# Denominators of 45 group halves by transpose and reduction on VectorE, in place of a matmul with ones

## The chip, the core and the metric

The kernel runs on one core of a Trainium2 chip. The metric is the device time of one execution in microseconds (us). The engines are TensorE (PE, with its weight loads PEld), VectorE (DVE), ScalarE (ACT), GpSimd (POOL) and SyncE (SP), which issues nearly all transfers. Each engine works through its own list of instructions in order, and semaphores order the lists against each other.

## The reference

A decoder block in fp32 on x (4, 1024, 512) with a context (4, 1024, 384). Three sublayers, each on a layernorm and each added to x:

- Self attention, 16 heads of 32. Scores of `x@Wi` against `x@Wo`, softmax over keys, times an aperture per query and an expression gate per key, and then normalized again by the sum over keys plus 1e-8:

```python
attn = attn_align * aperture.transpose(0, 2, 1)[..., :, None] * expression.transpose(0, 2, 1)[..., None, :]
attn = attn / (attn.sum(axis=-1, keepdims=True) + 1e-08)
```

  So for each head and query two sums over the keys are needed: that of the exps, and that of the exps weighted by the expression gate.
- Cross attention to the context, 16 heads of 32: an ordinary softmax, one sum of exps for each head and query.
- A network of 64 units with 16 inner relus each.

## The kernel before

**Units, halves and group halves.** There are eight attention units u: phase 0 (self attention) for the four batches, u = 0 to 3, then phase 1 (cross attention), u = 4 to 7. A unit has two halves hf of 512 queries, and a half has four groups g of four heads. The 64 triples (u, hf, g) are the group halves. Each has eight steps kt of 128 keys. `run` interleaves the steps with items from `beside`: projections, layernorms, output projections and the network of the neighbouring units. The order of every engine is the order in which the program writes it.

**One step.** `scores` (L633) computes two score tiles (two heads each, 128 keys x 1024, L641), and ACT turns each into an `e` tile by exp (L647). There are six buffers for `e`, so three steps' worth. In the next step `times` (L704) multiplies the `e` tiles with the values into `av` (L707).

**The sums over keys.** They come from three places:
- DVE adds `e` tiles over the eight steps into `es` (L669, L671): in phase 0 for the first two heads, in phase 1 of units 4 to 6 for both pairs. In phase 0 it also adds the gated exps of the first two heads into `eg` (L679; ACT starts it, L678).
- In phase 0 the other two heads get both sums from PE: rounds of four matmuls into `sm`, one round for two steps, with ones and the gate as weights (L717).
- For the group halves in the table `gated` (L625), DVE does the first 4 or 6 steps of those two heads, into `exa` (L685, L687) and `exb` (L692, started by ACT, L691), and PE takes these up in one round.

DVE's tiles are sums over steps only; the 128 keys of a step still lie in 128 partitions. `normalize` (L730) runs after the last step of a group half (it falls in step 0 of the next), copies `av` away (L733) and in phase 0 `sm` (L735), and one step later `add_up` (L743) sums over partitions: a round of four matmuls with `ones` as weights (L746), a copy (L747), and transfers through memory that bring the sums into a tile `c` of 128 partitions x 16 queries. Two steps later `divide` (L767) forms the reciprocals and sends them out and back, spread over partitions (`recb`), and two steps after that `multiply` (L795) applies them (L797). Unit 7 has a different split (`shared`, `added_up`).

**Buffers that matter.** `es0`, `es1`, `exa`, `exb`, `both` and `recb` have one buffer each; `eg` uses `es1`. The two tiles `cs_` are used in turn. PSUM has two score tiles, two banks `f` for everything else, and one each for `av` and `sm`. DVE frees a bank `f` where it adds the output projection to the residual (L891) or scales the values (L565); ACT frees most others.

Of the kernel before, what the change touches and what calls it, by code (L numbers as in the profile page):

```python
# [10 lines left out]
F32 = mybir.dt.float32  # L11
U32 = mybir.dt.uint32
AF = mybir.ActivationFunctionType
ALU = mybir.AluOpType
AX = mybir.AxisListType

P = 128
B, T, D = 4, 1024, 512
H, DH = 16, 32
NPR = H // 2  # L20
HG = 4
# [4 lines left out]
HALF = 512  # L26
M, INNER = 64, 16
# [12 lines left out]
NB = 32  # L40
# [29 lines left out]
def moderate_path(tc: tile.TileContext, a: dict, out: bass.AP, flag: bass.AP):  # L70
    nc = tc.nc
    x = a["x"]
    with ExitStack() as st:
        enter = st.enter_context
        const = enter(tc.tile_pool(name="mconst", bufs=1))
        dram = enter(tc.tile_pool(name="mdram", bufs=1, space=bass.MemoryType.DRAM))
# [4 lines left out]
        p1 = enter(tc.tile_pool(name="mp1", bufs=1))  # L81
        p2 = enter(tc.tile_pool(name="mp2", bufs=2))
# [35 lines left out]
        iap_d = [[dram.tile([H, HALF], F32, tag=f"iap_{b}_{i}", name="iap_d") for i in range(2)] for b in range(B)]  # L118
        sum1_d = [dram.tile([HG, HALF], F32, tag=f"sum1_{i}", name="sum1_d") for i in range(4)]
        sum2_d = [dram.tile([2, HG, HALF], F32, tag=f"sum2_{i}", name="sum2_d") for i in range(4)]  # L120
        rec_d = [dram.tile([HG, HALF], F32, tag=f"rec_{i}", name="rec_d") for i in range(4)]
        wout_d = dram.tile([P, NC, D], F32, name="wout_d")

# [2 lines left out]
        fixed = const.tile([P, 3], F32, name="fixed")  # L126
        ones, share, power = (fixed[:, i : i + 1] for i in range(3))
        pick = const.tile([P, 3], F32, name="pick")
        nc.gpsimd.memset(pick, 0.0)
        nc.gpsimd.memset(pick[:, 1:2], 1.0)  # L130
        for one, is_ in ((ones, 1.0), (power, -0.5), (share, 1.0 / M)):
            nc.gpsimd.memset(one, is_)

        NS = 2 * B * 2 * HG
        marks = const.tile([P, 2 * NS + B * NT], F32, name="marks")
# [56 lines left out]
        cs = p1.tile([P, 2, NC], F32, name="cs")  # L192
# [107 lines left out]
        av = pa.tile([P, HALF], F32, tag="av", name="av")  # L300
        nc.vector.memset(av, 0.0)
        sm = pa.tile([P, HALF], F32, tag="sm", name="sm")
        nc.vector.memset(sm, 0.0)


        cs_ = [const.tile([P, 2, 2, INNER], F32, name=f"cs{i}") for i in range(2)]
        for t in cs_:
            nc.gpsimd.memset(t, 0.0)

        S = {}  # L310
        crossing = []
# [62 lines left out]
        def after(steps, f, behind=False):  # L374

            soon.append((tick[0] + steps, behind, f))
# [236 lines left out]
        def attention(u, hf):  # L613

            ph, b = order[u]
            me = S[u]
            steps = []
            sums = 2 if ph == 0 else 1

            def shared(g):  # L620
                return ph == 0 or (u + 1 == len(order) and not (g == 1))

            added_up = {(0, 0): (0, 4), (0, 2): (0,), (0, HG - 1): (0, 4), (1, 0): (0,), (1, 2): (0,)} if u + 1 == len(order) else {}

            gated = {(0, 1, 0): 4, (0, 1, 1): 4, (0, 1, 2): 4, (0, 1, 3): 6, (1, 0, 0): 4, (1, 1, 0): 4, (1, 1, 1): 4, (1, 1, 2): 4, (1, 1, 3): 6, (2, 0, 0): 4, (2, 1, 0): 6, (2, 1, 1): 4, (2, 1, 2): 4, (2, 1, 3): 6, (3, 0, 0): 4, (3, 0, 3): 4, (3, 1, 0): 4, (3, 1, 1): 4, (3, 1, 3): 4}  # L625

            def apart(g):
                return 2 if u + 1 < len(order) else 3
# [100 lines left out]

            def normalize(g):  # L730
                i = (u * 2 + hf) * HG + g
                both = p1.tile([P, 2, HALF], F32, tag="both", name="both")
                nc.scalar.copy(me["q", hf][:, g, :], av)  # L733
                if shared(g):
                    nc.scalar.copy(both[:, 0, :], sm)  # L735
                    added = [me["es"][0][:, 0, :], me["es"][0][:, 1, :]]
                    if ph == 0:
                        added += [me["eg"][:, 0, :], me["eg"][:, 1, :]]
                else:
                    added = [me["es"][h // 2][:, h % 2, :] for h in range(HG)]  # L740
                after(1, lambda: add_up(g, i, both, added), behind=True)

            def add_up(g, i, both, added):  # L743

                for j, e in enumerate(added):
                    nc.tensor.matmul(sm[j * DH : j * DH + 1, :], lhsT=ones, rhs=e, start=True, stop=True)  # L746
                nc.scalar.copy(both[:, 1, :], sm)  # L747

                c, s1, s2 = cs_[i % 2], sum1_d[i % 4], sum2_d[i % 4]
                rows = both.rearrange("(j r) s q -> j r s q", r=DH)  # L750
                n = len(added)
                nc.sync.dma_start(s1[0:n], rows[0:n, 0, 1, :])
                if not shared(g):
                    nc.sync.dma_start(c[:, 0, 0, :], s1[0:n].rearrange("h (q e) -> (h q) e", e=INNER))
                else:
                    for k in range(sums):
                        nc.sync.dma_start(s2[k], rows[:, k, 0, :])
                    nc.sync.dma_start(
                        c[0:64, 0:sums, 0, :], s1[0:n].rearrange("(s h) (q e) -> (h q) s e", h=2, e=INNER)
                    )  # L760
                    for k in range(sums):
                        nc.sync.dma_start(
                            c[64:, k, :, :], s2[k].rearrange("(p h) (q e) -> (h q) p e", h=2, e=INNER)
                        )
                after(apart(g), lambda: divide(g, i, c))

            def divide(g, i, c):  # L767
                if shared(g):
                    both_ = p2.tile([P, sums, INNER], F32, tag="c2", name="both_")
                    nc.vector.tensor_tensor(both_, c[:, 0:sums, 0, :], c[:, 0:sums, 1, :], ALU.add)  # L770
                else:
                    both_ = c[:, 0:1, 0, :]
                if ph == 0:

                    den = p2.tile([P, INNER], F32, tag="den", name="den")
                    nc.vector.scalar_tensor_tensor(
                        den, both_[:, 0, :], 1e-8, me["iap", hf][:, g, :], ALU.mult, ALU.mult
                    )
                    nc.vector.tensor_tensor(den, den, both_[:, 1, :], ALU.add)
                else:  # L780
                    den = both_[:, 0, :]
                rec = p2.tile([P, INNER], F32, tag="rec", name="rec")
                nc.vector.reciprocal(rec, den)
                nc.vector.tensor_reduce(marks[:, i : i + 1], den, AX.X, ALU.add)
                nc.vector.tensor_reduce(marks[:, NS + i : NS + i + 1], rec, AX.X, ALU.add)
                nc.sync.dma_start(rec_d[i % 4].rearrange("j (q e) -> (j q) e", e=INNER), rec)

                all_ = p1.tile([P, HALF], F32, tag="recb", name="recb")
                for j in range(HG):
                    nc.sync.dma_start(  # L790
                        all_[j * DH : (j + 1) * DH, :], rec_d[i % 4][j : j + 1, :].to_broadcast([DH, HALF])
                    )
                after(apart(g) + (u + 1 == len(order) and g < 2), lambda: multiply(g, all_), behind=u + 1 < n or g < HG - 1)

            def multiply(g, all_):  # L795
                own = me["q", hf][:, g, :]
                nc.vector.tensor_tensor(own, own, all_, ALU.mult)  # L797
                me["divided", hf] = g
# [22 lines left out]
        def settle(u, hf, g):  # L821

            me = S[u]
            i = (u * 2 + hf) * HG + g
            rec = p1.tile([P, HALF], F32, tag="recb", name="recb")
            den = p1.tile([P, 2, HALF], F32, tag="both", name="den")[:, 0, :]
            few = p2.tile([P, INNER], F32, tag="rec", name="few")
            column = den.rearrange("p (b j) -> p b j", j=NB)[:, :, 0]

            def sums():  # L830
                me["by ones"](me["rest"], False, False)
                me["by ones"](me["e", NT - 1], False, True)

            def divide(part):
                cols, own = ts(part, HALF // 2), ts(part, INNER // 2)
                nc.vector.transpose(den[:, cols], sm[:, cols])
                nc.vector.reciprocal(few[:, own], column[:, own])
                nc.vector.transpose(rec[:, cols], few[:, own].unsqueeze(2).to_broadcast([P, INNER // 2, NB]))
                nc.vector.tensor_tensor(me["q", hf][:, g, cols], av[:, cols], rec[:, cols], ALU.mult)

            def look():
                nc.vector.tensor_reduce(marks[:, i : i + 1], column, AX.X, ALU.add)
                nc.vector.tensor_reduce(marks[:, NS + i : NS + i + 1], few, AX.X, ALU.add)

            return sums, divide, look
# [377 lines left out]
        p = pres[0]  # L1223
# [28 lines left out]
        sums, divide, look = settle(n - 1, 1, HG - 1)  # L1252
# [8 lines left out]
        h = [part for item in held[0]["h"] for part in item]  # L1261
# [671 lines left out]
```

## Time and profile before

| | us |
|---|---|
| median of three runs (2134.0 to 2136.43) | 2135.34 |
| the profiled execution | 2137.01 |
| its span, from first to last instruction | 2135.2 |
| PE busy | 2118.0 |
| DVE busy | 1677.9 |
| ACT busy | 1255.8 |

A busy share is a mean over stages; a view by stretches of time shows them apart. A group's row gives the line, engine, operation, result<-operands, shapes and count, then busy time and mean of one, then the engine's idle time just before and what ended it. Rows of the timeline give start and length in us. The start-to-start distance of DVE operations that follow each other is some 0.08 us under their length. A matmul in fp32 leaves two records.

### The profile page before, as it was taken

The numbers are of one execution on the slowest core, as the hardware profiler recorded it, in microseconds if no ns is written. First come the engines' busy times: TensorE is split into PE (matmuls) and PEld (weight loads), VectorE is DVE, ScalarE is ACT, GpSimd is POOL, SyncE is SP. The second block draws the span as 40 slices with busy tenths as digits, with TensorE's granted clock in tenths as the row PEclk, the third lists the DMA queues.
The fourth block names the chain that finished last, engine by engine and source line by source line (L and its number), as shares of the span: only waits on it lengthen the run. The fifth ranks groups of instructions, "written<-read, shape, count | busy, mean of one in ns | idle before, by whom it ended". The sixth has DMA issues, their size and how long they took to land.

```text
span 2135.2 us, 52477 instructions
## 1 busy us (share of the span) xinstructions
PE 2118.0 (99%) x22380; PEld 551.5 (26%) x22380; DVE 1677.9 (79%) x2468; ACT 1255.8 (59%) x1537; POOL 139.3 (7%) x184
## 2 busy tenths in 40 slices
PE   9999999999999999999999999999999999999998
PEld 5322222222222222222222222222222222222223
DVE  3477789888898888977889666887788778778887
ACT  0156555655556565565766666565655656567774
POOL 2000000040030100001000010000000000000001
PEclk9999999999999999999999999999999999999999
DMA  5422234132231212212222212231432213232231
GB/s 149 118 71 54 68 82 125 25 83 78 77 109 42 86 39 71 72 43 72 67 77 72 72 52 71 83 99 51 106 86 81 81 52 71 71 91 70 73 91 50
DMA packets 154495, 161.79 MB, mean 76 GB/s; under 512 B 47366, under 2 KB 93062, under 8 KB 153100
## 3 DMA queue, kind: packets, MB, share of 16 engines
q1 hardware_dynamic: 150188, 156.26, 25.4%
q8 instruction: 177, 2.90, 0.6%
q0 software_dynamic: 2080, 0.98, 0.3%
q10 hardware_dynamic: 1984, 1.12, 0.2%
q14 instruction: 66, 0.54, 0.1%
HBM read 115.53 MB, written 42.73 MB: 74 GB/s over the span
## 4 chain that ended last, share of the span: by engine, by line
PE 55%; DVE 1%; issue 0%; ACT 0%; DVEq 0%; ACTq 0%
PE f L107 19%; PE s L641 15%; PE av L707 14%; PE sm L746 2%; PE sm L717 2%; PE f L990 1%; PE f L641 1%; PE f L1068 0%; PE s L107 0%; DVE res L1076 0%; PE f L1024 0%; DVE es L671 0%; ACT e L647 0%; PE s L1068 0%; PE sm L697 0%
## 5 line engine op out<-in xcount | busy, mean ns | idle before, releaser
L647 ACT ACTIVATE e<-s 128x1024 f32<-128x1024 f32 x999 | 971.6, 1023 | 684.9 <-PE s L641 479.6
L671 DVE TENSOR_TENSOR es<-es,e 128x1024 f32<-128x1024 f32 x541 | 649.7, 1226 | 123.2 <-ACT e L647 121.9
L641 PE MATMUL s<-q,k 32*64 32x512 f32 x7992 | 589.3, 613 | 0.5 <-ACT e L647 0.2
L707 PE MATMUL av<-e,v 128*32 128x512 f32 x4096 | 548.2, 603 | 0.0
L107 PE MATMUL f<-xT,w 128*32 128x512 f32 x2816 | 333.7, 592 | 0.7 <-DVE xT L347 0.7
L679 DVE SCALAR_TENSOR_TENSOR eg<-e,sw,eg 128x512 f32<-128x512 f32 x448 | 315.2, 744 | 9.0 <-ACT eg L678 9.0
L669 DVE TENSOR_TENSOR es<-e 128x1024 f32<-128x1024 f32 x96 | 114.7, 1221 | 188.3 <-ACT e L647 176.6
L107 PE MATMUL f<-w,q 128*32 128x512 f32 x1984 | 238.6, 592 | 0.2
L641 PEld LDWEIGHTS s<-q,k 32*64 32x64 f32 x7992 | 129.1, 129 | 415.9 <-ACT e L647 199.5
L707 PEld LDWEIGHTS av<-e,v 128*32 128x32 f32 x4096 | 87.8, 108 | 402.9 <-issue 402.5
L107 PEld LDWEIGHTS f<-xT,w 128*32 128x32 f32 x2816 | 91.8, 110 | 211.4 <-issue 205.2
L107 PE MATMUL f<-w,xT 128*32 128x512 f32 x896 | 106.0, 592 | 0.6 <-DVE q L321 0.6
L107 PEld LDWEIGHTS f<-w,q 128*32 128x32 f32 x1984 | 64.7, 110 | 150.4 <-issue 142.2
L107 PE MATMUL f<-ctxT,w 128*32 128x512 f32 x768 | 92.3, 592 | 0.0
L107 PE MATMUL f<-w,ctxT 128*32 128x512 f32 x768 | 92.3, 592 | 0.0
L692 DVE SCALAR_TENSOR_TENSOR exb<-e,sw,exb 128x512 f32<-128x512 f32 x130 | 91.4, 743 | 0.0
L899 POOL TENSOR_TENSOR r<-res,bo_bc 128x512 f32<-128x512 f32 x32 | 40.9, 1279 | 747.0 <-DVE res L891 598.9
L717 PE MATMUL sm<-e,sw 128*2 128x512 f32 x688 | 89.5, 592 | 0.0
L327 POOL TENSOR_SCALAR rs<-fmv 128x4 f32<-128x4 f32 (+2 forms) x18 | 11.9, 659 | 833.6 <-DVE fmv L896 833.3
L746 PE MATMUL sm<-es,fixed 128*1 128x512 f32 x356 | 65.3, 591 | 0.0
L687 DVE TENSOR_TENSOR exa<-exa,e 128x1024 f32<-128x1024 f32 x46 | 55.9, 1216 | 0.0
L891 DVE TENSOR_TENSOR res<-f,res 128x512 f32<-128x512 f32 x62 | 42.4, 683 | 16.6 <-PE f L107 9.6
(293 smaller groups left out, 1354.7 us busy)
## 6 DMA issues: line engine op xcount, KB each, us to landing
recb<-rec_d SPq DMA_DIRECT2D x252, 64.0 KB
xT<-rows_d SPq DMA_DIRECT2D x60, 256.0 KB
rows_d<-r SPq DMA_DIRECT2D x60, 256.0 KB
w<-in_xattn_Wo SPq DMA_DIRECT2D x9, 1024.0 KB
w<-wout_d SPq DMA_DIRECT2D x8, 1024.0 KB
res<-in_x SPq DMA_DIRECT2D x32, 256.0 KB
x1b_d<-r SPq DMA_DIRECT2D x32, 256.0 KB
res<-x1b_d SPq DMA_DIRECT2D x32, 256.0 KB
```

Source lines behind the costliest of these rows:

```text
L107: nc.tensor.matmul(to[r], lhsT=lhsT[:, j, :] if len(lhsT.shape) == 3 else lhsT[:, r], rhs=rhs, **flags)
L641: nc.tensor.matmul(two[j][m : m + 64], lhsT=k[r, g, kt * P + m : kt * P + m + 64], rhs=q[r, g, :], start=True, stop=True,)
L647: nc.scalar.activation(e[:, h, :] if len(reads) == 1 else e[:, h.start, :], s, AF.Exp, scale=SCALE)
L669: nc.vector.tensor_tensor(me["es"][i], me["e", begin][i], es[i], ALU.add)
L671: nc.vector.tensor_tensor(me["es"][i], me["es"][i], es[i], ALU.add)
L679: nc.vector.scalar_tensor_tensor(eg, es[0][:, h, :], gate(kt), eg, ALU.mult, ALU.add)
L687: nc.vector.tensor_tensor(me["ep"], me["ep"], es[1], ALU.add)
L692: nc.vector.scalar_tensor_tensor(et, es[1][:, h, :], gate(kt, h), et, ALU.mult, ALU.add)
L707: nc.tensor.matmul(av[r, :], lhsT=me["v"][:, kt, HG * g + h, :], rhs=es[h // 2][:, h % 2, :], start=(kt == 0), stop=(kt == NT - 1),)
L717: nc.tensor.matmul(sm[j * DH : j * DH + sums, :], lhsT=lhsT, rhs=rhs, start=start, stop=stop)
L746: nc.tensor.matmul(sm[j * DH : j * DH + 1, :], lhsT=ones, rhs=e, start=True, stop=True)
L891: nc.vector.tensor_tensor(r, res["po"], r, ALU.add)
```

## The change

45 of the 64 group halves, listed in `flat`, leave out `add_up`. In its place `normalize` calls `fold`, which sums over the 128 partitions on DVE: `vector.transpose` turns blocks of 32x32, so that 32 keys lie beside each other in one partition, and `tensor_reduce` adds them up. It does so for a tile of two heads at once (1024 columns): one transpose and one reduction for each of two tiles. What is left, four partial sums for each query (one from each 32 partitions), goes to memory in one transfer and comes back in four, spread over 128 partitions, into the tile `four`, and `divide` adds the four up. The first tile is turned in the step in which `normalize` falls, the second one at the head of the next step, and `divide` comes two steps after that, as before. In phase 0 the sums of the last two heads, which lie in `sm`, take the same way as before, some instructions earlier. 29 of the 45 lie in phase 0, 16 in units 4 to 6.

The table `gated` shrinks from 19 entries to four, so that PE makes more L717 rounds in all 19: one more in 15 of them, where the entry goes, and one more in the four others, whose 6 becomes a 4. The tiles `cs_` go; `add_up` uses `four` as well. Two memsets at the start change place.

```diff
+        parts_d = [dram.tile([P, HG, INNER], F32, tag=f"parts_{i}", name="parts_d") for i in range(4)]
...
-        cs_ = [const.tile([P, 2, 2, INNER], F32, name=f"cs{i}") for i in range(2)]
-        for t in cs_:
-            nc.gpsimd.memset(t, 0.0)
...
-            gated = {(0, 1, 0): 4, (0, 1, 1): 4, (0, 1, 2): 4, (0, 1, 3): 6, (1, 0, 0): 4, (1, 1, 0): 4, (1, 1, 1): 4, (1, 1, 2): 4, (1, 1, 3): 6, (2, 0, 0): 4, (2, 1, 0): 6, (2, 1, 1): 4, (2, 1, 2): 4, (2, 1, 3): 6, (3, 0, 0): 4, (3, 0, 3): 4, (3, 1, 0): 4, (3, 1, 1): 4, (3, 1, 3): 4}
+            gated = {(0, 1, 3): 4, (1, 1, 3): 4, (2, 1, 0): 4, (2, 1, 3): 4}
+
+            flat = ((0, 0, 0), (0, 0, 1), (0, 0, 3), (0, 1, 0), (0, 1, 1), (0, 1, 2), (0, 1, 3), (1, 0, 0), (1, 0, 3), (1, 1, 0), (1, 1, 1), (1, 1, 2), (1, 1, 3), (2, 0, 0), (2, 0, 3), (2, 1, 0), (2, 1, 1), (2, 1, 2), (2, 1, 3), (3, 0, 0), (3, 0, 1), (3, 0, 2), (3, 0, 3), (3, 1, 0), (3, 1, 2), (3, 1, 3), (4, 0, 0), (4, 0, 1), (4, 0, 2), (4, 0, 3), (4, 1, 0), (5, 0, 1), (5, 0, 2), (5, 1, 0), (6, 0, 1), (6, 0, 2), (6, 1, 0), (0, 0, 2), (1, 0, 2), (2, 0, 2), (4, 1, 2), (5, 0, 0), (5, 1, 2), (6, 0, 0), (6, 1, 2))
...
             def normalize(g):
                 i = (u * 2 + hf) * HG + g
+                nc.scalar.copy(me["q", hf][:, g, :], av)
+                if (u, hf, g) in flat:
+                    return fold(g, i)
                 both = p1.tile([P, 2, HALF], F32, tag="both", name="both")
-                nc.scalar.copy(me["q", hf][:, g, :], av)
...
+            def fold(g, i):
+                tiles = [me["eg"], me["es"][0]] if ph == 0 else [me["es"][0], me["es"][1]]
+                at = (1, 0) if ph == 0 else (0, 1)
+                parts = p1.tile([P, 2, 2, INNER], F32, tag="parts", name="parts")
+                own, to = parts_d[i % 4], p1.tile([P, 2, 4, INNER], F32, tag="four", name="four")
+                if ph == 0:
+                    both = p1.tile([P, 2, HALF], F32, tag="both", name="both")[:, 0, :]
+                    nc.scalar.copy(both, sm)
+                    rows, s2 = both.rearrange("(j r) q -> j r q", r=DH), sum2_d[i % 4]
+                    for k in range(2):
+                        nc.sync.dma_start(s2[k], rows[:, k, :])
+                    for k in range(2):
+                        nc.sync.dma_start(
+                            to[64:, k, 0:2, :], s2[k].rearrange("(p h) (q e) -> (h q) p e", h=2, e=INNER)
+                        )
+
+                def turn(k):
+                    w = p1.tile([P, 2, INNER, NB], F32, tag="exa" if ph == 0 else "both", name="turned")
+                    nc.vector.transpose(w, tiles[k].rearrange("p h (i e) -> p h e i", e=INNER))
+                    nc.vector.tensor_reduce(parts[:, at[k]], w, AX.X, ALU.add)
+
+                def rest():
+                    turn(1)
+                    nc.sync.dma_start(own, parts.rearrange("p k h e -> p (k h) e"))
+                    if ph == 0:
+                        for k in range(2):
+                            for h in range(2):
+                                nc.sync.dma_start(
+                                    to[h * DH : (h + 1) * DH, k],
+                                    own[:, 2 * k + h, :].rearrange("(a i) e -> i a e", i=DH),
+                                )
+                    else:
+                        for h in range(HG):
+                            nc.sync.dma_start(
+                                to[h * DH : (h + 1) * DH, 0], own[:, h, :].rearrange("(a i) e -> i a e", i=DH)
+                            )
+
+                turn(0)
+                after(1, rest)
+                after(1 + apart(g), lambda: divide(g, i, to))
...
             def divide(g, i, c):
-                if shared(g):
+                if (u, hf, g) in flat:
                     both_ = p2.tile([P, sums, INNER], F32, tag="c2", name="both_")
-                    nc.vector.tensor_tensor(both_, c[:, 0:sums, 0, :], c[:, 0:sums, 1, :], ALU.add)
+                    r = slice(0, 64 if ph == 0 else P)
+                    nc.vector.tensor_reduce(
+                        both_[r], c[r, 0:sums].rearrange("p k a e -> p k e a"), AX.X, ALU.add
+                    )
+                    if ph == 0:
+                        nc.vector.tensor_tensor(both_[64:], c[64:, :, 0, :], c[64:, :, 1, :], ALU.add)
```

More of the change, by code (lines that the diff above doesn't have):

```diff
@@ L128, in moderate_path @@
         pick = const.tile([P, 3], F32, name="pick")
+        for one, is_ in ((ones, 1.0), (power, -0.5), (share, 1.0 / M)):
+            nc.gpsimd.memset(one, is_)
         nc.gpsimd.memset(pick, 0.0)
         nc.gpsimd.memset(pick[:, 1:2], 1.0)
-        for one, is_ in ((ones, 1.0), (power, -0.5), (share, 1.0 / M)):
-            nc.gpsimd.memset(one, is_)
         NS = 2 * B * 2 * HG
@@ L747, in add_up @@
                 nc.scalar.copy(both[:, 1, :], sm)
-                c, s1, s2 = cs_[i % 2], sum1_d[i % 4], sum2_d[i % 4]
+                c, s1, s2 = p1.tile([P, 2, 4, INNER], F32, tag="four", name="four"), sum1_d[i % 4], sum2_d[i % 4]
                 rows = both.rearrange("(j r) s q -> j r s q", r=DH)
@@ L762, in add_up @@
                         nc.sync.dma_start(
-                            c[64:, k, :, :], s2[k].rearrange("(p h) (q e) -> (h q) p e", h=2, e=INNER)
+                            c[64:, k, 0:2, :], s2[k].rearrange("(p h) (q e) -> (h q) p e", h=2, e=INNER)
                         )
@@ L767, in divide @@
             def divide(g, i, c):
-                if shared(g):
+                if (u, hf, g) in flat:
                     both_ = p2.tile([P, sums, INNER], F32, tag="c2", name="both_")
-                    nc.vector.tensor_tensor(both_, c[:, 0:sums, 0, :], c[:, 0:sums, 1, :], ALU.add)
+                    r = slice(0, 64 if ph == 0 else P)
[4 more added lines that the diff above has]
+                        nc.vector.tensor_tensor(both_[64:], c[64:, :, 0, :], c[64:, :, 1, :], ALU.add)
+                elif shared(g):
+                    both_ = p2.tile([P, sums, INNER], F32, tag="c2", name="both_")
+                    nc.vector.tensor_copy(both_[0:64], c[0:64, 0:sums, 0, :])
+                    nc.vector.tensor_tensor(both_[64:], c[64:, 0:sums, 0, :], c[64:, 0:sums, 1, :], ALU.add)
                 else:
```

## The prediction

> **What bounds the kernel now.** I read the busy shares first, then the stages, then one group boundary on each engine, then the waits. The busy shares:
>
> ```profile
> PE 2118.0 (99%) x22380; PEld 551.5 (26%) x22380; DVE 1677.9 (79%) x2468; ACT 1255.8 (59%) x1537; POOL 139.3 (7%) x184
> ```
>
> PE runs without a hole; the 17 us in which it is idle lie nearly all at the start and in the tail. Split at the first score of each attention unit (units 1, 4, 5 and 6 shown; columns: length, then busy PE, PEld, DVE, ACT, POOL, then clock, DMA share, GB/s):
>
> ```profile
> 371.00:644.00 273.00, 272.66 (x2906) 67.71 (x2898) 231.54 (x353) 160.74 (x196) 47.87 (x67) 1.00 0.27 77
> 1177.00:1416.00 239.00, 239.00 (x2540) 59.45 (x2536) 166.11 (x199) 147.80 (x171) 11.38 (x12) 1.00 0.26 75
> 1416.00:1660.00 244.00, 243.94 (x2580) 60.26 (x2582) 196.18 (x274) 147.66 (x171) 5.61 (x6) 1.00 0.28 80
> 1660.00:1904.00 244.00, 243.85 (x2580) 60.80 (x2576) 195.02 (x270) 147.12 (x171) 5.62 (x6) 1.00 0.28 79
> ```
>
> PE fills every unit at full clock; DVE has 41 us over in unit 1, 73 in unit 4, 48 and 49 in units 5 and 6. So a matmul round taken off PE shortens the kernel by its length, unless what replaces it makes DVE late enough to hold PE. What a round is worth stands in PE's timeline at a boundary between two group halves:
>
> ```profile
> 613.32 1.11 PE L641 MATMUL s<-q,k 32*64 32x512 f32 x16
> 614.37 0.60 PE L746 MATMUL sm<-es,fixed 128*1 128x512 f32 x2
> 614.38 0.60 PE L746 MATMUL sm<-eg,fixed 128*1 128x512 f32 x2
> 614.79 0.60 PE L746 MATMUL sm<-es,fixed 128*1 128x512 f32 x2
> 614.81 0.60 PE L746 MATMUL sm<-eg,fixed 128*1 128x512 f32 x2
> 615.22 1.04 PE L707 MATMUL av<-e,v 128*32 128x512 f32 x8
> ```
>
> Four matmuls (two records each) run beside each other; the next kind starts 0.85 us after them. The L717 rounds are the same: 609.77 to 610.63, 0.86 us. At the same boundary DVE stands idle, for its next operand comes one step later:
>
> ```profile
> 609.69 1.41 DVE L679 SCALAR_TENSOR_TENSOR eg<-e,sw,eg 128x512 f32<-128x512 f32 x2
> 615.58 1.23 DVE L669 TENSOR_TENSOR es<-e 128x1024 f32<-128x1024 f32 x1 [4.49 <-ACT e L647]
> ```
>
> Over all boundaries that is the L669 row below: 188.3 us of idle time.
>
> ```profile
> L669 DVE TENSOR_TENSOR es<-e 128x1024 f32<-128x1024 f32 x96 | 114.7, 1221 | 188.3 <-ACT e L647 176.6 <-PE sm L746 11.7
> L692 DVE SCALAR_TENSOR_TENSOR exb<-e,sw,exb 128x512 f32<-128x512 f32 x130 | 91.4, 743 | 0.0
> L687 DVE TENSOR_TENSOR exa<-exa,e 128x1024 f32<-128x1024 f32 x46 | 55.9, 1216 | 0.0
> L347 DVE STREAM_TRANSPOSE xT<-xT 128x512 f32<-128x512 f32 x60 | 37.2, 676 | 0.0
> ```
>
> **PE, part by part.** (1) 45 group halves lose their add_up round (L746): 45 rounds off. (2) The gated table shrinks from 19 entries (fifteen 4s, four 6s) to four 4s. An ungated phase-0 group half has 4 sm rounds (L717), a 4 has 3, a 6 has 2. Before, the table saved 15 + 8 = 23 rounds; after, 4. So 19 rounds come back. Net 26 rounds off, 104 matmuls, which is also what counting both programs gives. 26 x 0.855 = 22.2 us, all on the path, as PE is the path.
>
> **DVE.** Off: 53 adds into exa (x 1.217 = 64.5) and 106 gated sums into exb (x 0.743 = 78.8), 143 us, all in phase 0. On: 90 transposes of 128x1024 and 90 reductions of 128x1024 to 32 sums. The transposes: 445 ns at 256 columns (L836), 676 at 512, so 0.90 ns a column and 1.14 us at 1024, if the 64-byte stride of the read is free. The reductions: 170 ns at 16 columns (L785), 319 at 160 (L1280), so 1.03 ns a column and 1.21 us; taking L784's 111 ns as the start gives 1.44 ns and 1.56 us. With 0.25 us for the longer sum in divide, a fold costs 2 x (1.14 + 1.21) + 0.25 = 4.95 us. 29 folds in phase 0 add 144 us where 143 go: even. 16 folds in units 4 to 6 add 79 us: unit 5 rises from 196 to 221 us of some 240, unit 4 from 166 to 196. No unit saturates, so I book nothing on the path. What hides it: the boundary idle (4.49 us in the place shown), since the first transpose follows the last add of its group and the second comes before the next L669. There 609.69 + 1.41 + 4.7 ends at 615.8 against 615.58: a fifth of a microsecond late. The short gaps before a fold's next L669 are 0 (200.62), 0.63 (1481.69), 0.64 (1725.36), 1.20 (1756.26), 1.29 (1242.48) and 1.35 (989.24): DVE gets up to 4.7 us late there and catches up within the group, where it has 5 to 6 us over. (Those of 0.83 at 651.30 and 1.74 at 378.44 follow gated 6s that become 4s, so they widen.)
>
> How late may it be? Each e tile is one of six, three steps; the exp three steps on waits for DVE's read. The tightest such pair before is in a gated group half:
>
> ```profile
> 597.42 1.41 DVE L692 SCALAR_TENSOR_TENSOR exb<-e,sw,exb 128x512 f32<-128x512 f32 x2
> ```
>
> ```profile
> 599.88 1.02 ACT L647 ACTIVATE e<-s 128x1024 f32<-128x1024 f32 x1
> ```
>
> The read ends at 598.83, 1.05 us before the exp that takes its buffer, and PE has no hole. That chain of four gated operations a step is what the change removes from 15 group halves. So its tightest places go, and lateness of 3 to 5 us at six boundaries takes their place, against some two steps (7.5 us) of cover. The evacuations L891, L1076 and the transpose L347 behind such a boundary come 1 to 3 us later; the banks they free are wanted about two steps on. I book 1 us of PE waits for all this (0 to 4).
>
> [...] No row of before has a long DVE read with a 64-byte stride; the nearest are the same instruction read in order (L347, L836). [...]
>
> **Bounds of the transposes.** Low: 1.14 us, in-order slope. High, from the farthest row: the reciprocals cost 253 ns at 16 columns and 549 at 64 (L537, strided at both ends), 6.2 ns a column, 6.3 us at 1024. I take 1.14, as the row of the same instruction is nearest.
>
> **ACT, SP.** ACT loses 45 copies of sm (0.59) and 30 starts of exb (0.72): 48 us off an engine at 59%. Its start of eg (L678) now waits for DVE's transpose of the old eg in place of PE's round; at the boundary shown the transpose would end at 612.2 and L678 starts at 616.35. SP gets 135 DMAs more: 45 writes of parts (0.34 like rec_d), 180 reads (0.62 like the cs reads), less 45 sum_d writes (0.5), 16 short and 29 long cs reads: some 80 us of issue on a queue that issues for about 550 and stands waiting for the sums anyway. Behind the parts write, which waits for DVE, stand the four reads, the rec_d and recb of the same group half, and rows_d and xT transfers:
>
> ```profile
> 621.16 0.63 SPq L758 DMA_DIRECT2D cs<-sum_d  x1
> 621.88 1.41 SPq L762 DMA_DIRECT2D cs<-sum_d  x2
> 623.38 2.13 SPq L341 DMA_DIRECT2D xT<-rows_d  x4
> ```
>
> From the second reduction: 0.34 issue, 1.7 to landing (1482.88 to 1484.56 before), 4 x 0.7 for the reads, about 1.6 for the last: 6.4 us. divide comes two steps later, 7.4 to 9.2 us. It holds; missed, DVE would wait 1 to 2 us in a place with no hurry.
>
> **Sum.** The profiled execution took 2137.0 us (span 2135.2 and 1.8 around it). 2137.0 - 22.2 + 1 = 2115.8; it stood 1.7 us above the median of the runs, so the median comes to 2114.1. I say 2114.
>
> **Rivals.**
> (B) DVE's lateness costs real PE waits, with transposes at twice the in-order slope, 2.28 us. At 2 x (2.28 + 1.21) + 0.25 = 7.2 us a fold no unit saturates, but the six short boundaries are 6 to 7 us late, at the edge of the cover: 0.5 to 2 us each, 3 to 12 in all: 2116 to 2125. For it: short gaps. Against: the tightest pair of before held at 1.05 us.
> (C) Slower, by saturated DVE: units 5 and 6 have (48 - 4) / 5 = 8.7 us for each fold, unit 4 has (239 - 166 - 5) / 6 = 11.3, phase 0 (183 + 143 - 9) / 29 = 10.9. Beyond 8.7 each microsecond a fold costs 10 us: 10 x (C - 8.7) eats the 22.2 at C = 10.9, that is transposes of 4.1 us. At 4.6 us each (C = 11.9) the loss is 32 + 4 + 29: about 2178. At the high end of 6.3 it would pass 2300. Against: nothing on DVE but a reciprocal has such a slope.
> (D) The change doesn't free PE, since scores wait for the exps at a boundary: 45 rounds become waits and 19 are added, 16 us slower, 2151. For it: PEld waits for ACT before many scores. Against: those waits lie under running matmuls, and ACT is idle 2.62 us before the exp at 614.52.
>
> **How the numbers follow.** Forecast 0.77 (own range 2112 to 2117), B 0.11, C 0.07, D 0.02, some mix that lands within 0.2% (4.3 us, about what a measurement here can tell) 0.03. Faster 0.88, same 0.03, slower 0.09. The range 2111 to 2125 leaves out C, D and the mix, and its lower end lets the rounds be worth 0.95 us.
>
> **What the profile after would show.** PE some 2096 us busy, still 99%; L746 with 180 matmuls fewer (360 records); the transposes at 1.14 us and the reductions at 1.2 to 1.6; L669's idle time down from 188 to below 60 us; DVE at 83%; no PE wait on ACT exp or on f banks over 1 us. Transposes over 2 us, or exps that wait for DVE, would make the forecast wrong.

## The result and the profile after

The changed kernel takes 2148.78 us (median of four runs, 2147.89 to 2149.87), the kernel before 2134.78 us beside it: a ratio of 1.0063 with an interval of 1.005 to 1.0077. It is 14 us slower, where 21 us faster was forecast. The profiled execution took 2147.89 us, its span is 2146.1 us against 2135.2. The page's busy shares after:

```profile
PE 2108.4 (98%) x22172; PEld 544.0 (25%) x22172; DVE 1834.2 (85%) x2542; ACT 1217.2 (57%) x1462; POOL 134.5 (6%) x182
```

PE has 208 records fewer, which is what 26 rounds of four matmuls leave, and 37.7 us of idle time in place of 17.2. The work went, and waits came. DVE's groups (busy time and mean ns, then idle time before and what ended it):

```profile
L763 DVE STREAM_TRANSPOSE turned<-es 128x1024 f32<-128x1024 f32 x61 | 117.5, 1927 | 0.9
L764 DVE TENSOR_REDUCE parts<-turned 128x32 f32<-128x1024 f32 x90 | 109.8, 1220 | 3.1
L763 DVE STREAM_TRANSPOSE turned<-eg 128x1024 f32<-128x1024 f32 x29 | 56.0, 1930 | 0.6
L669 DVE TENSOR_TENSOR es<-e 128x1024 f32<-128x1024 f32 x96 | 114.4, 1218 | 22.2 <-ACT e L647 19.8
```

The reductions take the 1.2 us forecast for them; the transposes take 1.93 us, not 1.14. The boundary idle before L669 fell from 188.3 to 22.2 us. PE's longest waits (total us, times, longest):

```profile
PE s L641 <- ACT e L647: 8.7, 3, 4.5
PE f L1120 <- DVE res L1128: 5.7, 3, 2.8
PE f L1120 <- DVE g L1109: 4.4, 2, 2.2
PE f L107 <- DVE v L563: 2.4, 1, 2.4
```

These are seven gaps that the kernel before did not have: 4.49 us (at 399.5) and 4.01 (678) before scores, 2.37 (208) before a projection, and 2.71, 2.20, 2.78 and 2.19 before output products in units 5 and 6 (L1120, before L1068). The windows show what follows five of them (length, busy PE, PEld, DVE, ACT, POOL, then the granted clock, DMA share, GB/s):

```profile
211.10:214.50 3.40, 3.40 (x28) 0.53 (x24) 2.17 (x3) 0.10 (x1) 0.00 (x0) 0.50 0.14 38
402.30:409.00 6.70, 5.00 (x24) 1.10 (x28) 6.70 (x9) 2.96 (x3) 0.00 (x0) 0.50 0.14 39
682.20:689.00 6.80, 6.54 (x32) 1.29 (x32) 6.80 (x10) 2.14 (x3) 0.00 (x0) 0.50 0.05 17
1709.60:1712.90 3.30, 3.30 (x25) 0.72 (x28) 3.08 (x8) 1.03 (x2) 0.00 (x0) 0.50 0.53 202
1832.50:1835.80 3.30, 3.30 (x21) 0.33 (x17) 3.27 (x6) 0.00 (x0) 0.00 (x0) 0.50 0.06 6
```

TensorE's granted clock is 0.50 there, and matmuls are longer: the eight records of `av` in one step take 1.94 us at 405.91 and 1.07 at 411.21, at full clock again. So about half of the busy PE time in these rows, 10.8 us, is lost as well (an estimate from the rows). Unit by unit, with the gaps of each unit, the rounds that are fewer or more on PE in it (net, each 0.855 us; a fold of a unit's last group half takes its round out of the next unit) and half of the busy half-clock time, in us:

| unit | rounds | gaps | half clock | sum | measured |
|---|---|---|---|---|---|
| 0 | -2: -1.7 | 2.4 | 1.7 | +2.4 | +2.7 |
| 1 | -2: -1.7 | 4.5 | 2.5 | +5.3 | +6.0 |
| 2 | -2: -1.7 | 4.0 | 3.3 | +5.6 | +6.3 |
| 3 | -3: -2.6 | | | -2.6 | -3.7 |
| 4 | -7: -6.0 | | | -6.0 | -5.6 |
| 5 | -5: -4.3 | 4.9 | | +0.6 | +2.9 |
| 6 | -5: -4.3 | 5.0 | 3.3 | +4.0 | +3.6 |
| 7 | | | | 0 | +0.5 |
| all | -22.2 | 20.8 | 10.8 | +9.4 | +12.7 |

The stage ahead of the first exp was 2.0 us shorter (101.9 for 103.9), which brings the units' +12.7 to the span's +10.9 (but for rounding). Some 3 us of the units' 12.7 are not told by these gaps and the clock; one more gap, of 0.69 us at 1659.0 in unit 5, is part of them.

**The two longest gaps.** They follow back through four engines. PE's, ACT's and DVE's timelines of after around the first of them, one row each:

```profile
404.00 1.98 PE L641 MATMUL s<-q,k 32*64 32x512 f32 x8 [4.49 <-ACT e L647]
```

```profile
402.92 1.02 ACT L647 ACTIVATE e<-s 128x1024 f32<-128x1024 f32 x1 [6.02 <-DVE eg L679]
```

```profile
377.41 1.22 DVE L764 TENSOR_REDUCE parts<-turned 128x32 f32<-128x1024 f32 x1
...
398.89 0.36 DVE L814 TENSOR_REDUCE both__3625<-four 64x32 f32<-64x128 f32 x1 [14.73 <-DMA four<-parts_d]
```

PE waits for an exp, the exp for DVE to free an `e` tile, and DVE stands in `divide` (L814) for 14.7 us, until the sums are back from memory; `parts` was ready at 378.6. SP's queue, the transfers in the order of issue, and SP's longest wait in 360 to 402:

```profile
375.06 1.10 SPq L755 DMA_DIRECT2D sum_d<-both  x2
376.78 1.28 SPq L757 DMA_DIRECT2D four<-sum_d  x2
378.11 0.59 SPq L408 DMA_DIRECT2D xin<-in_x  x1
378.75 0.50 SPq L148 DMA_DIRECT2D w<-wout_d  x1
379.29 2.29 SPq L916 DMA_DIRECT2D res<-in_x  x4
381.68 5.06 SPq L112 DMA_DIRECT2D w<-in_attn_Wv  x4
388.42 0.34 SPq L768 DMA_DIRECT2D parts_d<-parts  x1
395.45 2.01 SPq L772 DMA_DIRECT2D four<-parts_d  x4
```

```profile
SPq L755 <- ACT both L752: 17.6, 1, 17.6
```

`fold` writes `sum_d` out in step 0, and in the program that write stands ahead of the next unit's loads (x, the residual, two weights, some 4 MB). SP stands 17.6 us at it for ACT's copy of `sm`. In the kernel before, the first and the last of these loads were issued at 359.73 and 370.29:

```profile
359.73 0.42 SPq L410 DMA_DIRECT2D xin<-in_x  x1
...
370.29 2.71 SPq L112 DMA_DIRECT2D w<-in_attn_Wv  x4
```

Now the first is issued at 378.11, behind the write. So `parts_d` is issued behind 4 MB of loads, ten us after `parts` was ready, and takes 7.0 us to be back as something that can be read (388.42 to 395.45). The gap of 4.01 us at 678 has the same chain, with a wait of 14.0 us in `divide`. The next waits of L814, 8.0 us and less, held up no score by more than 0.2 us.

**The shorter gaps.** DVE and PE around the one at 1458.7:

```profile
1455.32 1.91 DVE L763 STREAM_TRANSPOSE turned<-es 128x1024 f32<-128x1024 f32 x1
1457.27 1.22 DVE L764 TENSOR_REDUCE parts<-turned 128x32 f32<-128x1024 f32 x1
1458.41 2.35 DVE L669 TENSOR_TENSOR es<-e 128x1024 f32<-128x1024 f32 x2
1460.67 1.28 DVE L1128 TENSOR_TENSOR res<-f,res 128x512 f32<-128x512 f32 x2
```

```profile
1455.46 1.20 PE L1120 MATMUL f<-outs,g 64*128 64x512 f32 x4
1456.59 1.11 PE L641 MATMUL s<-q,k 32*64 32x512 f32 x16
1457.63 1.06 PE L707 MATMUL av<-e,v 128*32 128x512 f32 x8
1461.41 1.72 PE L1120 MATMUL f<-outs,g 64*128 64x512 f32 x4 [2.71 <-DVE res L1128]
```

PE fills both banks `f` with output products at 1455.5 and wants them back one step later. DVE empties them with L1128 (before L1076), which stands behind the second transpose, its reduction and two adds, and starts at 1460.67, 2.7 us too late for PE. The gaps of 2.78 and 2.37 us are of this kind too. In the gaps of 2.20 and 2.19 us PE waits for no bank but for an operand: DVE forms the last sum of `g` (L1109) behind the fold.

### The profile page after: what moved, and what is told of

The parts are those of the page before. It is cut to its first block, busy times and chain, and to the rows that moved or that the text cites. A ratio compares the mean times of both kernels' runs of the same rounds, so it can differ in the third digit from the quotient of the medians.

```text
span 2146.1 us, 52123 instructions
## 1 busy us (share of the span) xinstructions
PE 2108.4 (98%) x22172; PEld 544.0 (25%) x22172; DVE 1834.2 (85%) x2542; ACT 1217.2 (57%) x1462; POOL 134.5 (6%) x182
## 4 chain that ended last, share of the span: by engine, by line
PE 88%; DVE 5%; DMA 3%; issue 2%; SPq 1%; ACT 1%; ACTq 0%; DVEq 0%
PE f L107 35%; PE s L641 23%; PE av L707 21%; PE sm L717 5%; DVE es L671 1%; PE s L107 1%; DVE turned L763 1%; DMA parts_d<-parts 1%; PE sm L789 1%; DMA res<-in_x 1%; PE f L1042 1%; DVE parts L764 1%; PE f L641 1%; ACT e L647 1%; PE f L1120 0%
## 5 line engine op out<-in xcount | busy, mean ns | idle before, releaser
L641 PE MATMUL s<-q,k 32*64 32x512 f32 x7992 | 595.7, 616 | 8.9 <-ACT e L647 8.7
L669 DVE TENSOR_TENSOR es<-e 128x1024 f32<-128x1024 f32 x96 | 114.4, 1218 | 22.2 <-ACT e L647 19.8
L717 PE MATMUL sm<-e,sw 128*2 128x512 f32 x960 | 125.0, 592 | 0.0
L763 DVE STREAM_TRANSPOSE turned<-es 128x1024 f32<-128x1024 f32 x61 | 117.5, 1927 | 0.9
L764 DVE TENSOR_REDUCE parts<-turned 128x32 f32<-128x1024 f32 x90 | 109.8, 1220 | 3.1
L325 POOL TENSOR_SCALAR rs<-fmv 128x4 f32<-128x4 f32 (+2 forms) x18 | 10.9, 605 | 836.3 <-DVE fmv L948 836.0
L763 DVE STREAM_TRANSPOSE turned<-eg 128x1024 f32<-128x1024 f32 x29 | 56.0, 1930 | 0.6
L1109 DVE SCALAR_TENSOR_TENSOR g<-ring,units,g 128x256 f32<-128x256 f32 x105 | 50.1, 478 | 2.7 <-ACT ring L1102 1.8
```

The source lines that it names most:

```text
L641: nc.tensor.matmul(two[j][m : m + 64], lhsT=k[r, g, kt * P + m : kt * P + m + 64], rhs=q[r, g, :], start=True, stop=True,)
L669: nc.vector.tensor_tensor(me["es"][i], me["e", begin][i], es[i], ALU.add)
L717: nc.tensor.matmul(sm[j * DH : j * DH + sums, :], lhsT=lhsT, rhs=rhs, start=start, stop=stop)
L763: nc.vector.transpose(w, tiles[k].rearrange("p h (i e) -> p h e i", e=INNER))
L764: nc.vector.tensor_reduce(parts[:, at[k]], w, AX.X, ALU.add)
L1109: nc.vector.scalar_tensor_tensor(res["g"], res["hid"], units[:, 2, h - 1 : h], res["g"], ALU.mult, ALU.add)
```

## The experiments

Theory S (queue order): what costs most is that the transfers of `sum_d` moved ahead of the loads on SP. Rival T (DVE's work): the 1.93 us transposes make DVE late wherever a fold falls. The first four kernels were timed beside 31 runs of the kernel before (median 2135.71), the last four beside eight (2136.82). Line numbers of experiments differ from those of after by up to four.

**1. The `sum_d` transfers one step later.** They are issued at the head of `rest`, so behind the loads.

```diff
-                    for k in range(2):
-                        nc.sync.dma_start(s2[k], rows[:, k, :])
...
+                def others():
+                    for k in range(2):
+                        nc.sync.dma_start(s2[k], rows[:, k, :])
...
                 def rest():
+                    if ph == 0:
+                        others()
                     turn(1)
```

> The phase-0 transfers of the sums in sm (two writes, two reads) are issued one step later, behind the loads for the next unit instead of ahead of them; nothing else changes. Theory (SP order): in the changed kernel SP stands in front of these writes for 17.6 us until ScalarE has copied sm, the loads of 4 MB go out at 378 us instead of 360, the partial sums queue behind them, and divide waits 14.7 and 14.0 us. Without that the PE gaps of 4.49 and 4.01 us go and the two half-clock stretches of 6.8 us behind them (3.4 us of loss each): 15 us less than the changed kernel's 2148.8, about 2134. Rival (VectorE simply has too much to do): no change, 2147 to 2150.

Measured: 2131.86 us (10 runs), ratio 0.9985 (0.9975 to 0.9995), 17 us less than the changed kernel had in its own runs. SP's queue in this run:

```profile
357.72 0.43 SPq L408 DMA_DIRECT2D xin<-in_x  x1
...
371.41 1.76 SPq L112 DMA_DIRECT2D w<-in_attn_Wv  x4
375.37 1.10 SPq L757 DMA_DIRECT2D sum_d<-both  x2
378.07 1.34 SPq L759 DMA_DIRECT2D four<-sum_d  x2
379.50 0.54 SPq L772 DMA_DIRECT2D parts_d<-parts  x1
381.17 1.74 SPq L776 DMA_DIRECT2D four<-parts_d  x4
```

The loads go out at 357.7 again, `parts_d` at 379.5, and its readers follow after 1.7 us. Both long gaps and their half-clock stretches are gone; the five shorter gaps stay (2.40, 2.71, 2.17, 2.79, 2.17). Theory S holds for about half of the 35 us that the forecast missed, and rival T is needed for the rest.

**2. No transposes and reductions.** All else of the fold stays.

```diff
+        parts = const.tile([P, 2, 2, INNER], F32, name="parts")
+        nc.vector.memset(parts, 1.0)
...
-                parts = p1.tile([P, 2, 2, INNER], F32, tag="parts", name="parts")
...
                 def turn(k):
-                    w = p1.tile([P, 2, INNER, NB], F32, tag="exa" if ph == 0 else "both", name="turned")
-                    nc.vector.transpose(w, tiles[k].rearrange("p h (i e) -> p h e i", e=INNER))
-                    nc.vector.tensor_reduce(parts[:, at[k]], w, AX.X, ALU.add)
+                    pass
```

> All 90 transposes and 90 reductions are left out, the partial sums are constants (so the denominators are wrong); all transfers and the order on SP stay. Theory (two causes: VectorE late behind the folds, and SP order): the gaps behind the folds (2.37, 2.71, 2.20, 2.78, 2.19 us) and their half-clock stretches go, 17 us in all, but the two waits for transfers stay: about 2131. Rival (VectorE's load is the whole cause): all stalls go and PE shows its 26 rounds of 0.855 us: 2113. Rival (the rounds were never worth 0.855 us): 2125 or more with no gaps left.

Measured: 2131.68 us (10 runs), ratio 0.9982 (0.9972 to 0.9991). DVE's and PE's waits:

```profile
395.72 0.36 DVE L813 TENSOR_REDUCE both__3571<-four 64x32 f32<-64x128 f32 x1 [14.77 <-DMA four<-parts_d]
```

```profile
PE s L643 <- ACT e L649: 9.0, 4, 4.5
```

With 268 us less on DVE the wait in `divide` is as long as before (14.77 for 14.73), and the gaps before scores are 4.53 and 4.11 us. The five shorter gaps are gone. So DVE's load makes the shorter gaps and has no part in the longer ones: each of the two causes takes some 17 us away by itself.

**3. The transposes read in order.** The blocks are cut along the columns, so that each element read lies beside the last one.

```diff
-                    nc.vector.transpose(w, tiles[k].rearrange("p h (i e) -> p h e i", e=INNER))
+                    nc.vector.transpose(w, tiles[k].rearrange("p h (c j) -> p h c j", j=NB))
```

> Each transpose reads its 1024 columns in order instead of at a stride of 64 bytes (the sums then belong to other queries, so the result is wrong); everything else is the same. If the stride is what makes the transpose cost 1.93 us, it falls to 1.1 to 1.2 us, a fold to 5.0 us, each short boundary is 1.5 us less late, and the gaps of 2.2 to 2.8 us shrink to about 1 us, some without a half-clock stretch: about 2136, the two waits for transfers remaining. If 1024 columns cost 1.93 us in any order (a longer instruction has its own price), nothing changes: 2148 to 2150.

Measured: 2136.76 us (10 runs), ratio 1.0008 (0.9998 to 1.0018); 12 us less than the changed kernel.

```profile
L763 DVE STREAM_TRANSPOSE turned<-es 128x1024 f32<-128x1024 f32 x61 | 75.5, 1237 | 0.9
```

The stride of the read costs 0.69 us of 1.93. With 1.24 us the shorter gaps shrink to 0.99, 1.53, 0.80, 1.53 and 0.80, and only one of them is followed by a half-clock stretch. The long gaps stay (5.02 and 3.11), and two gaps of 0.87 and 1.34 us come (at 950 and 2079), whose cause was not looked for.

**4. Four boundaries not folded**, those ahead of the output products.

```diff
-            flat = (... (5, 1, 0), (6, 1, 0), (5, 0, 0), (6, 0, 0) ...)
+            flat = (the 41 others)
```

> Four group halves of phase 1, (5,0,0), (5,1,0), (6,0,0), (6,1,0), go back to the round on PE; 41 are left. Theory: PE's gaps of 2.71, 2.20, 2.78 and 2.19 us at the output products of the network (they wait for a bank that VectorE frees late, or for its last sum) go with two half-clock stretches (1.7 us each), 13.3 us, and 4 rounds of 0.855 us come back, 3.4: about 2139. Rival (the gaps have another cause, such as the transfers): the gaps stay and the time rises by 3.4 us to 2152.

Measured: 2137.79 us (10 runs), ratio 1.001 (1.0 to 1.0019). The gaps before L1120 are gone; 2.37 (208), 4.38 (399) and 4.83 (679) are left, each with its half clock. Four folds that take 3.4 us off PE cost 11 us more than they give.

**5. Both remedies**: experiment 1, and five boundaries not folded, those of experiment 4 and (0, 0, 2), which makes the gap at 208.

> The sums issued later, as in the first experiment, and 40 folds: (5,0,0), (5,1,0), (6,0,0), (6,1,0) and (0,0,2) go back to the round on PE. If each PE gap has its own cause and the gains add up: 2131.9 with the sums later, less 9.8 us of gaps and 3.4 of half clock in phase 1, less 2.4 and 1.7 at (0,0,2), plus five rounds of 0.855: 2119. If VectorE's load as a whole makes PE wait, other gaps open and it stays above 2125.

Measured: 2117.59 us (2116.27 to 2118.43, four runs), ratio 0.991 (0.9893 to 0.9926): faster than both kernels.

```profile
PE 2098.0 (99%) x22212; PEld 541.2 (26%) x22212; DVE 1805.4 (85%) x2518; ACT 1219.1 (58%) x1467; POOL 134.4 (6%) x182
L669 DVE TENSOR_TENSOR es<-e 128x1024 f32<-128x1024 f32 x96 | 114.4, 1218 | 40.4 <-ACT e L647 37.8 <-PE sm L793 2.5
```

PE has no gap that the kernel before does not have, and no half clock between the start and the tail. Against before, phase 0 is 7.2 us shorter (8 rounds net: 6.8 us), units 4, 5 and 6 are 5.8, 2.5 and 2.3 us shorter (7, 3 and 3 rounds: 6.0, 2.6 and 2.6). So 21 rounds took 17.8 us, 0.85 each; the rest of the 19.8 us of span is a start stage that was 2.1 us shorter. That rest need not come of the change: in experiment 8, whose edit leaves the start as it is, the stage is 2.3 us shorter too. DVE is as busy as in after, 85%.

**6. As 5, with (0, 0, 2) folded.**

> As the kernel with 40 folds, but (0,0,2) stays a fold. PE's gap of 2.4 us at about 208 us (it waits for a bank that VectorE frees behind the second transpose) and the half-clock stretch of 3.4 us behind it stay: 2122, that is 3 us over the kernel with 40 folds. If that gap has another cause, the two kernels differ by the round of 0.855 us alone, and this one is the faster.

Measured: 2121.16 us (2118.27 to 2123.74, four runs), ratio 0.9927 (0.991 to 0.9944), 3.6 us more than experiment 5. The gap is back (2.35 us at 207.7), and a half-clock stretch of 3.41 us after it. The fold takes 0.86 us off PE and opens a gap that costs several times as much.

**7. As 5, with three more folds**, at boundaries with idle time before L669 but with DVE products queued behind them.

```diff
+            flat += ((4, 1, 3), (5, 1, 1), (5, 1, 3))
```

> As the kernel with 40 folds, with three other group halves folded: (4,1,3), (5,1,1), (5,1,3). Where VectorE has idle time before its next first add is 2.4, 1.5 and 2.4 us in the kernel before, less than a fold of 6.5 takes. If only an evacuation that PE wants soon makes PE wait, these cost nothing and three rounds go: 2116. If the missing idle time decides, each opens a gap of 2 to 4 us with its half-clock stretch: 2124 to 2131.

Measured: 2121.15 us (four runs), ratio 0.9929 (0.9912 to 0.9946), between the two expectations. Its new gaps on PE, all in the second half of unit 5, and DVE between the first and the second:

```profile
1581.22 1.07 PE L107 MATMUL f<-w,q 128*32 128x512 f32 x8 [0.98 <-DVE res L947]
1609.67 1.07 PE L107 MATMUL f<-xT,w 128*32 128x512 f32 x8 [2.20 <-DVE xT L345]
1640.51 1.92 PE L1046 MATMUL f<-xn,win 128*32 128x256 f32 x28 [1.60 <-DVE xn L345]
```

```profile
1580.47 0.69 DVE L947 TENSOR_TENSOR res<-f,res 128x512 f32<-128x512 f32 x1 [5.55 <-DMA res<-x1b_d]
...
1588.09 1.88 DVE L765 STREAM_TRANSPOSE turned<-es 128x1024 f32<-128x1024 f32 x1
...
1607.13 2.48 DVE L345 STREAM_TRANSPOSE xT<-xT 128x512 f32<-128x512 f32 x4
```

The first gap is a residual that lands late; DVE waits 5.55 us for it (in experiment 5 it waits 2.7 us before the same addition, and the profile does not name what for), and no run tells whether a fold made it later. From there DVE has no idle time, with the fold at 1588 among its work, until it hands over xT 20 us later, too late for PE by 2.20 us. The gaps come to 4.8 us against 2.6 us for three rounds, and the start stage of this run, with 6.83 us of half clock in it, was 1.5 us longer. So it seems that the idle time at a fold's own boundary does not price it: lateness can be carried on for several steps, to a product (here a transposed input) that PE wants soon. How much each of the three folds has in it was not told apart.

**8. The kernel before with the short `gated` table and no folds.** 19 rounds come back onto PE, and the additions that DVE and ACT made in their place go.

```diff
-            gated = {(0, 1, 0): 4, (0, 1, 1): 4, (0, 1, 2): 4, (0, 1, 3): 6, (1, 0, 0): 4, (1, 1, 0): 4, (1, 1, 1): 4, (1, 1, 2): 4, (1, 1, 3): 6, (2, 0, 0): 4, (2, 1, 0): 6, (2, 1, 1): 4, (2, 1, 2): 4, (2, 1, 3): 6, (3, 0, 0): 4, (3, 0, 3): 4, (3, 1, 0): 4, (3, 1, 1): 4, (3, 1, 3): 4}
+            gated = {(0, 1, 3): 4, (1, 1, 3): 4, (2, 1, 0): 4, (2, 1, 3): 4}
```

> The kernel before with the short table of four gated group halves, and no folds: 19 rounds come onto PE, 143 us go off VectorE. If a round is worth 0.855 us on the path, 2135.7 + 16.2 = 2152. If rounds in sm are partly hidden, or VectorE's load held PE up in the kernel before, less: 2136 to 2148.

Measured: 2145.39 us (five runs), ratio 1.0039 (1.0025 to 1.0053). Units 0 to 3 are 4.2, 3.1, 3.1 and 1.2 us longer, 11.6 us for 19 rounds, 0.61 each in place of 0.855 (the medians of the runs are 8.6 us apart). The time from the start of one kind of matmul to the start of the next shows why. In these units the rounds into `sm` take 15.3 us more, 0.80 each, and the scores of units 1 to 3 take 3.4 us less. In the kernel before, some scores of gated group halves take up to 1.9 us in place of 1.04. The same step of unit 3, before and here:

```profile
928.11 2.00 PE L641 MATMUL s<-q,k 32*64 32x512 f32 x16
```

```profile
936.23 1.11 PE L641 MATMUL s<-q,k 32*64 32x512 f32 x16
```

So a gated group half had cost PE some time that shows as no gap. The folds have such a cost too: against experiment 8, experiment 5 spends 23.1 us less on the rounds of units 0 to 3, but 3.6 us more on their scores and 0.7 us more on their `av` matmuls. What holds these matmuls up was not tested.

## Why the prediction was wrong

- **"26 x 0.855 = 22.2 us, all on the path": right.** The records are gone, and in experiment 5, without the gaps, 21 rounds were worth 0.85 us each. For the 19 that come back alone, experiment 8 gives 0.80, and 0.61 after what the scores gain.
- **SP, "a queue that issues for about 550 and stands waiting for the sums anyway": the step that failed, 17 of the 35 us by which the forecast missed.** The queue's length was counted, and what stands behind the `parts` write was listed, but not what the moved `sum_d` writes would stand in front of: "some instructions earlier" is past 4 MB of loads at the end of a unit. They wait for ACT in step 0, and the next unit's loads, the first of which had gone out 18 us earlier, now wait with them and are then in the way of `parts_d`. The 6.4 us from second reduction to landing became 20 us (378.6 to 398.9).
- **"It holds; missed, DVE would wait 1 to 2 us in a place with no hurry": wrong as a price.** DVE waited 14.7 and 14.0 us, with the adds that free `e` behind it in its order, and the exps 6.0 us.
- **The transposes at 1.14 us: mis-sized.** They take 1.93, in order 1.24 (experiment 3), so a fold costs 2 x (1.93 + 1.22) + 0.25 = 6.55 us, not 4.95. The 1.93 us lie inside the bounds (1.14 to 6.3). The read at 64 bytes takes 1.56 times as long as the one in order. Rival B's factor of two was the author's supposition; no run shows it.
- **"The banks they free are wanted about two steps on": the other step that failed, for the other 17 us.** Behind (5, 0, 0), (6, 0, 0) and (0, 0, 2) they are wanted after one step, and behind (5, 1, 0) and (6, 1, 0) it is the operand `g` that PE wants. Experiment 4 shows it for the four folds of phase 1 together, experiment 6 for (0, 0, 2). I carried one cover over to all places, where each needs its own: from PE's last use of a bank to its next. "1 us of PE waits (0 to 4)" was 12.3 us, and half clock took 5.0 us beside it.
- **The price of a gap was its length only.** The half clock after the gaps added 10.8 us in all.
- **The rivals.** B had DVE's lateness as a cost, but not its places, and that its 3 to 12 us come near the 12.3 is luck. It put the waits at the six boundaries with 0 to 1.35 us of idle time; only the one at 200.62, behind (0, 0, 2), is followed by a gap of over 0.6 us, and the four other gaps stand where the kernel before has 3.19 and 3.71 us of idle time before L669. C did not come: no unit saturates DVE, and experiment 5 gains at the same 85%. D did not come: in experiment 5 PE waits for exps 0.5 us in all. That the loss would start on SP was no rival at all.
- **The signs named.** PE busy 2108 for 2096 (half clock, 10.8 us by the estimate above), L669's idle time 22 (below 60, right), DVE 85% for 83%; "no PE wait ... over 1 us" fell, and "exps that wait for DVE" named the trace of the long gaps.

## What to carry to other kernels

When a transfer moves up on a queue that issues in order, as SP's did here, ask what it waits for and which loads it now stands ahead of; the length of the queue says nothing about it. When work goes into an engine's idle time, follow each product queued behind it to the engine that wants it, and count the steps until then place by place. Don't price a gap on TensorE by its length alone: in the changed kernel the gaps of 2.2 to 4.5 us cost up to 3.3 us more by half clock, and some of them nothing more; the next section has what went with it.

## What the hardware showed that was not expected

- **Half clock after short gaps.** Over after and the experiments, all eight gaps of over 3 us within the attention units were followed by 6.83 us at a granted clock of 0.5; of 13 gaps of 2.1 to 2.8 us, eight were followed by 3.41 us of it; of those below 2 us, one (1.53 us). What decides was not shown; what went with it in these runs is how a gap lies in time. In each run's record of the granted clock the stretches begin whole multiples of 3.41 us apart (in the changed kernel 56, 138, 439 and 475 of them behind the one at 211). Counted in pieces of 3.41 us, laid end to end from where a stretch begins, over the time at full clock between start and tail, each of the 15 with 1.89 us of idle time or more was followed by half clock and none with 1.34 us or less; between them two were (1.53 and 1.72) and four were not (1.55 to 1.78). In the changed kernel alone, those with 1.93, 2.19, 2.37, 2.73 and 3.41 us were, and those with 1.55 and 1.67 were not. All five gaps of 2.1 to 2.8 us without half clock were cut in two by the border of such a piece (in the changed kernel 2.71 into 1.67 and 1.04, and 2.20 into 1.55 and 0.65).
- **A strided read on DVE.** The transpose of 128x1024 in fp32 takes 1.93 us where its elements lie 64 bytes apart (the changed kernel) and 1.24 us in order (experiment 3); the reduction behind it takes 1.22 us in both runs.
- **A small write behind loads.** The write of `parts` took 7.0 us to its readers' issue (388.42 to 395.45) behind some 4 MB of loads, and 1.7 us (379.50 to 381.17 in experiment 1) without them.
